# Graph convolutions on one Trainium2 core: a group's features are made behind the next tile's sums, and the slot products get a third PSUM bank

## The chip, the cores and the metric

The kernel runs on one core of a Trainium2 chip. The metric is device time in microseconds (us) of one execution. Before the change three runs took 6908.93, 6929.65 and 6957.83 us, so the median is 6929.65 us. Engines are called as in the profile: PE is the matrix engine (PEld its weight loads), DVE the vector engine, ACT the scalar engine, POOL the engine that issues the gathers, SP the engine that issues most plain DMAs.

## The reference, cut to what matters

There are 12500 nodes with 128 features and 200000 edges sorted by target. First an attention layer over the edges adds its result to `x`. Then three graph convolutions follow, each with the same edges; the change touches only these:

```python
def _gcn_conv(x, W, b, src, dst, norm, num_nodes):
    h = x @ W
    msg = h[src] * norm[:, None]
    out = jax.ops.segment_sum(msg, dst, num_segments=num_nodes)
    return out + b
...
h = _gcn_conv(x, W1, b1, src, dst, norm, n)
h = _batch_norm(jax.nn.relu(h), g1, beta1)
h = _gcn_conv(h, W2, b2, src, dst, norm, n)
h = _batch_norm(jax.nn.relu(h), g2, beta2)
h = _gcn_conv(h, W3, b3, src, dst, norm, n)
return _batch_norm(h, g3, beta3)
```

`norm` is the product of one factor per source and one per target node, and each node has an edge to itself. The first convolution widens to 256 features (`W1` is 128x256), the others have 128. The batch norm needs mean and variance over all nodes, so a convolution must be finished before the next starts.

## The kernel before

The first half of the time (up to about 3560 us of the profiled span) is the attention; while it runs, the edges are also sorted into slots. Then come the three convolutions (`convolutions`, L1389), each one call of `run` in `conv_slots` (L1239). All matrices are fp32; each fp32 matrix product is two matmul records in the trace.

**Tiles and blocks.** Target nodes are cut into 106 tiles of 118. Nine tiles are a block (`TB`), so there are 12 blocks. Source nodes are cut into 98 segments of 128, and 14 segments are a take-group (`SG`), so a block has 7 take-groups. For each tile and segment there are 13 slots, that is, up to 13 edges from that segment into that tile; the edges that find no slot (up to 768 a tile) are fetched row by row.

**take(b)** (L1264) fills the slots of block b. For each take-group, in sub-groups of 4, 4, 4 and 2 segments, DVE builds a one-hot matrix `go` (L1273, three buffers), PE multiplies it with the segment's features, which lie in SBUF (`gp`, L1276, two PSUM banks), and ACT copies the product to `stage` (L1278, two buffers). When a take-group is done, two DMAs on ACT's queue write it to a block `m` in DRAM (L1280).

**reduce(b)** (L1283) adds up a block's tiles. For each tile three DMAs on SP's queue bring its slots back, now with the slots as partitions (`mr`, L1297, loaded three tiles ahead, four buffers); six gathers on POOL fetch the rows of the slotless edges (`rows`, L1312, by the helper in L150, five buffers); DVE builds the one-hot matrix `oh` of their targets (L1316, two buffers); and PE adds 10 products of `mr` (L1320) and 6 of `rows` (L1322) into a part of the PSUM tile `zp`, after one product of the tile's own rows `tg` with an identity (`own`, L1195).

**finish** (L1191) walks through a group of three tiles (`GN`) that share one `zp` bank. After the third tile DVE multiplies `zp` by the target factors into `zt` (L1199), and `use` makes the group's features of it. In the first convolution `use1` (L1398) multiplies `zt` on PE with both halves of W1 (L1403, 2 products of 354 columns, so four records), ACT adds the bias and applies relu (L1404, twice), DVE takes statistics (L1344, twice), and a DMA on ACT's queue stores the second half (`hb_d`, L1406). In the second and third convolution `use` (L1409) is one ACT instruction that reads `zt` (L1411) and one statistics instruction.

**Order.** Take-groups of block b alternate with the tiles of block b-1: the loop in L1328 gives `reduce` 0, 1, 3, 5, 6, 8 and 10 steps by the end of take-group 0 to 6, where the first step only issues loads. So the written order is: take-group, then one or two tiles, and so on; the third tile of a block's last group comes at the end of the block. What each engine really runs is not exactly the written order. A planner in the framework takes the written order as the priority and its own guess of durations, and lays out one fixed order for each engine. In the trace, for example, 12 `gp` matmuls stand between matmuls of one tile's sum.

**PSUM before.** [...]one constant (`tb`), two each for `gp`, `zp` and `bank` (the pool `ps`, L1246; `bank` is used by the products with W1 and by the transforms between convolutions). Seven are taken.

Of the kernel before, what the change touches and what calls it, by code (L numbers as in the profile page):

```python
# [8 lines left out]
FP = mybir.dt.float32  # L9
# [5 lines left out]
PSUM = bass.MemoryType.PSUM  # L15
# [3 lines left out]
D = 128  # L19
# [15 lines left out]
TN = 118  # L35
# [14 lines left out]
def tile_gnn(ctx: ExitStack, tc: tile.TileContext, x, src, dst, ea, eaT, wqkvT, weT, w1, w2, w3, par, out):  # L50
# [102 lines left out]
    with ExitStack() as s:  # L153
        once = s.enter_context(tc.tile_pool(name="once", bufs=1))
        sr = s.enter_context(tc.tile_pool(name="sr", bufs=3))
        ps = s.enter_context(tc.tile_pool(name="ps", bufs=2, space=PSUM))
# [507 lines left out]
    def fast():  # L664
# [234 lines left out]
        with ExitStack() as s:  # L899
# [7 lines left out]
            wk = s.enter_context(tc.tile_pool(name="wk", bufs=2))  # L907
# [280 lines left out]
                              dinv_d[t0 * TN:(t0 + n) * TN].unsqueeze(0).to_broadcast([P, n * TN]))  # L1188
            return tg, db

        def finish(wk, t0, n, zp, use, ps, own_, add):  # L1191

            tg, db = own_
            for i in range(n):
                nc.tensor.matmul(zp[:, i, :], tg[:, i, :], ident[:TN, :TN], start=True, stop=False)  # L1195
                add(i)
                yield
            zt = wk.tile([P, GN * TN], FP, name="zt")
            nc.vector.tensor_tensor(zt[:, :n * TN], zp[:, :n].rearrange("p a b -> p (a b)"), db[:, :n * TN],  # L1199
                                    op=ALU.mult)  # L1200
            use(wk, t0, n, zt[:, :n * TN], ps)

        def pools(s, *names):
            return [s.enter_context(tc.tile_pool(name=n, bufs=b)) for n, b in names]
# [4 lines left out]
        def conv_rows(s):  # L1209


            ew, ga, wk = pools(s, ("ew", 1), ("ga", 3), ("wk", 2))
            ps = s.enter_context(tc.tile_pool(name="ps", bufs=2, space=PSUM))
            srcA = ew.tile([P, NTT, JJ], I32, name="srcA")
            dlA = ew.tile([P, NTT, JJ], BF, name="dlA")
            nc.sync.dma_start(srcA, sw_d.rearrange("t (p j) -> p t j", j=JJ))
            nc.sync.dma_start(dlA, dlb_d.rearrange("t (p j) -> p t j", j=JJ))

            def run(table, use, ready):
                for g in range(NS // SG):  # L1220
                    ready(g)
                for t0, n in groups(NTT, GN):
                    zp = ps.tile([P, GN, TN], FP, name="zp")

                    def add(i):
                        rows = ga.tile([P, JJ, D], FP, name="rows")
                        for j in range(JJ):
                            gather(rows[:, j, :], table, srcA[:, t0 + i, j:j + 1])
                        oh = wk.tile([P, JJ, TN], FP, name="oh")
                        one_hot(oh, dlA[:, t0 + i, :])  # L1230
                        for j in range(JJ):
                            nc.tensor.matmul(zp[:, i, :], rows[:, j, :], oh[:, j, :], start=False, stop=(j == JJ - 1))

                    for _ in finish(wk, t0, n, zp, use, ps, own(wk, table, t0, n), add):
                        pass

            return ps, run

        def conv_slots(s):  # L1239
# [4 lines left out]
            blocks = s.enter_context(tc.tile_pool(name="blocks", bufs=3, space=DRAM))  # L1244
            tb = s.enter_context(tc.tile_pool(name="tb", bufs=1, space=PSUM))
            ps = s.enter_context(tc.tile_pool(name="ps", bufs=2, space=PSUM))  # L1246
            nums = tb.tile([P, TN], FP, name="nums")
            nc.vector.tensor_copy(nums, iota_f[:, :TN])
            TS = TB * SB

            def run(table, use, ready):
                every = [(b, g) for b in range(NBK) for g in range(NS // SG)]
                gis = []

                def load_slots(k):

                    for b, g in every[len(gis):k]:
                        gi = gy.tile([P, TB, SG * SB], U8, name="gi")
                        nc.sync.dma_start(gi.rearrange("p t k -> p (t k)"),
                                          gi_d[b, g].rearrange("t k -> (t k)").unsqueeze(0)  # L1260
                                          .to_broadcast([P, TS * SG]))
                        gis.append(gi)

                def take(b, m):  # L1264
                    for g in range(NS // SG):
                        load_slots(b * (NS // SG) + g + 2)
                        if b == 0:
                            ready(g)
                        stage = sg.tile([TS, SG, D], FP, name="stage")
                        gv = gis[b * (NS // SG) + g].rearrange("p t (s k) -> p s t k", k=SB)  # L1270
                        for a, n in groups(SG, 4):
                            go = gx.tile([P, 4, TB, SB], FP, name="go")
                            nc.vector.tensor_scalar(go[:, :n], gv[:, a:a + n], iota_q, None, op0=ALU.is_equal)  # L1273
                            gp = ps.tile([TS, 4, D], FP, name="gp")
                            for i in range(n):
                                nc.tensor.matmul(gp[:, i, :], go[:, i].rearrange("p t k -> p (t k)"),  # L1276
                                                 hs[:, g * SG + a + i, :], start=True, stop=True)
                            nc.scalar.copy(stage[:, a:a + n, :], gp[:, :n, :])  # L1278
                        for x, y in ((0, 112), (112, TS)):
                            nc.scalar.dma_start(m[x:y, g * SG:(g + 1) * SG, :], stage[x:y])  # L1280
                        yield

                def reduce(b, m):  # L1283

                    tiles = range(b * TB, min(NTT, (b + 1) * TB))
                    mrs, owns = {}, {}

                    def load(t):
                        if t not in tiles:
                            return  # L1290
                        if t % GN == 0:
                            owns[t] = own(wk, table, t, min(GN, NTT - t))
                        k = (t - b * TB) * SB
                        mv = m[k:k + SB].rearrange("k s d -> (k s) d")
                        mr = mrs[t] = mt.tile([P, RC, D], FP, name="mr")
                        for x, y, r in ((0, 112, RC), (112, LP, RC), (LP, LP + 1, LR)):
                            nc.sync.dma_start(mr[x:y, :r], mv[x * RC:(y - 1) * RC + r]  # L1297
                                              .rearrange("(p c) d -> p c d", c=r))

                    for a in range(AH):  # L1300
                        load(tiles[0] + a)
                    yield
                    for t0 in range(tiles[0], tiles[-1] + 1, GN):
                        n = min(GN, NTT - t0)
                        zp = ps.tile([P, GN, TN], FP, name="zp")

                        def add(i):
                            t = t0 + i
                            load(t + AH)
                            rows = ga.tile([P, JO, D], FP, name="rows")  # L1310
                            for j in range(JO):
                                gather(rows[:, j, :], table, srcO[:, t, j:j + 1])  # L1312
                            mr = mrs.pop(t)
                            oh = wk.tile([P, RC + JO, TN], FP, name="oh")
                            sh = list(oh.shape)
                            nc.vector.tensor_tensor(oh, nums.unsqueeze(1).to_broadcast(sh),  # L1316
                                                    dlS[:, t, :].unsqueeze(2).to_broadcast(sh), op=ALU.is_equal)
                            for j in range(RC):
                                q = LP + (j < LR)
                                nc.tensor.matmul(zp[:, i, :], mr[:q, j, :], oh[:q, j, :], start=False, stop=False)  # L1320
                            for j in range(JO):
                                nc.tensor.matmul(zp[:, i, :], rows[:, j, :], oh[:, RC + j, :], start=False,  # L1322
                                                 stop=(j == JO - 1))

                        yield from finish(wk, t0, n, zp, use, ps, owns.pop(t0), add)

                taken = None
                for b in range(NBK + 1):  # L1328
                    tiles = reduce(b - 1, taken) if b else iter(())
                    if b < NBK:  # L1330
                        taken = blocks.tile([TS, NS, D], FP, name="m")
                        done = 0
                        for g, _ in enumerate(take(b, taken)):
                            while done < g * (TB + 1) * SG // (NS - SG):
                                next(tiles, None)
                                done += 1
                    for _ in tiles:
                        pass

            return ps, run  # L1340

# [161 lines left out]
```

## Time and profile before

| | |
|---|---|
| median of 3 runs | 6929.65 us (6908.93 to 6957.83) |
| profiled execution | 6996.49 us; its span from the first to the last instruction is 6994.6 us |
| mean granted PE clock over the span | 0.762 |
| PE busy / DVE / ACT / POOL | 64% / 47% / 22% / 50% of the span |
| first convolution | about 3560 to 4640 us of the span |
| second, with the transform of its input | about 4650 to 5790 us |
| third, with the transform of its input | about 5810 to 6920 us |

The profile is one execution; each row of it gives busy time and the idle time of an engine just before the instructions of a row, with what ended most of that idle time. "issue" means that the engine waited for nothing that the profile shows. "remote", or "another core or an unknown queue", means that the wait ended with a semaphore's update for which no instruction was found near in time; there is only one core here. Ends of matmuls are modelled, their starts are recorded. The DMA column is the mean busy share of the core's 16 DMA engines.

### The profile page before, as it was taken

What the parts mean: (1) busy time and instruction counts of PE and PEld (TensorE: products, weight loads), DVE (VectorE), ACT (ScalarE), POOL (GpSimd) and SP (SyncE); (2) the same over time, 40 slices, a digit from 0 to 9 for tenths busy, and PEclk for the clock granted to TensorE, in tenths of its full rate; (3) what the DMA queues carried; (4) which work ended last, traced back from release to release, by engine and by line L of the source; (5) the groups of instructions that cost most, each with busy time, mean ns of one, the idle gap of its engine ahead of it and who ended that gap; (6) DMA issues with size and microseconds to landing.
All of it is one profiled execution on the core that took longest, in us unless ns stands there. A gap on an engine that the chain in (4) does not pass through costs nothing.

```text
span 6994.6 us, 79497 instructions
## 1 busy us (share of the span) xinstructions
PE 4480.9 (64%) x28140; PEld 4142.4 (59%) x28140; DVE 3297.8 (47%) x6145; ACT 1521.5 (22%) x2637; POOL 3518.1 (50%) x3617
## 2 busy tenths in 40 slices
PE   5455555555555555566557777786777776777776
PEld 2455544544444545555557777776777676767775
DVE  7344445565655666557523333352333334333334
ACT  2222222332222322222211211111111111111110
POOL 1444545455454554556435555525555553555552
PEclk9666666666666666667678888898888888888887
DMA  6434443433333433434377777766777776777776
GB/s 179 108 94 109 107 110 101 102 103 97 94 102 93 105 98 103 104 100 115 76 183 211 200 204 202 206 204 188 197 198 198 193 198 179 200 200 195 194 202 160
DMA packets 617743, 1051.02 MB, mean 150 GB/s; under 512 B 191467, under 2 KB 432043, under 8 KB 617233
## 3 DMA queue, kind: packets, MB, share of 16 engines
q1 hardware_dynamic: 434383, 478.08, 27.5%
q0 software_dynamic: 142608, 348.39, 19.0%
q10 hardware_dynamic: 40348, 219.37, 9.1%
q8 instruction: 228, 3.74, 0.2%
q14 instruction: 176, 1.44, 0.1%
HBM read 773.19 MB, written 272.26 MB: 149 GB/s over the span
## 4 chain that ended last, share of the span: by engine, by line
PE 41%; another core or an unknown queue 19%; DVE 16%; issue 12%; DMA 4%; ACT 2%; POOL 1%; SPq 1%; DVEq 0%; ACTq 0%; POOLq 0%
PE gp L1276 12%; PE zp L1320 10%; PE zp L1322 5%; PE qe L1061 5%; PE acc L1120 5%; DVE sc L1065 2%; DVE vals L1110 2%; DVE A L717 2%; DVE kv L1062 2%; DVE oh L1116 1%; PE sm L1072 1%; DVE A L718 1%; ACT stage L1278 1%; PE bank L1382 1%
## 5 line engine op out<-in xcount | busy, mean ns | idle before, releaser
L150 POOL DMA_INDIRECT rows<-t_d,srcO x1908 | 1834.9, 962 | 1605.8 <-issue 492.5
L150 POOL DMA_INDIRECT kv<-kv_d,srcA x1696 | 1678.9, 990 | 1638.1 <-DVE vals L1110 891.2
L1276 PE MATMUL gp<-hs,go 128*117 128x128 f32 x7056 | 1042.1, 305 | 553.3 <-issue 261.8
L1276 PEld LDWEIGHTS gp<-hs,go 128*117 128x117 f32 x7056 | 953.6, 207 | 613.9 <-issue 391.4
L1061 PE MATMUL qe<-qt,oht 128*128 128x128 f32 x3392 | 855.6, 418 | 581.3 <-DVE kv L1062 408.8
L1061 PEld LDWEIGHTS qe<-qt,oht 128*128 128x128 f32 x3392 | 769.8, 309 | 637.5 <-issue 381.5
L1278 ACT COPY stage<-gp 117x512 f32<-117x512 f32 x1008 | 514.4, 534 | 2442.7 <-PE gp L1276 823.1
L1316 DVE TENSOR_TENSOR oh<-nums,dlS 128x1888 f32<-128x1888 f32 x318 | 674.2, 2120 | 755.7 <-PE zp L1320 313.7
L1320 PE MATMUL zp<-oh,mr 128*128 128x118 f32 x6360 | 904.3, 288 | 182.8 <-issue 141.4
L1320 PEld LDWEIGHTS zp<-oh,mr 128*128 128x128 f32 x6360 | 834.2, 204 | 217.2 <-issue 189.0
L1273 DVE TENSOR_SCALAR go<-gi,iota_q 128x468 f32<-128x468 uint8 x1008 | 441.6, 460 | 931.4 <-remote 359.7
L1120 PE MATMUL acc<-vals,oh 128*118 128x137 f32 x3392 | 559.7, 335 | 175.4 <-ACT vals L1112 102.4
L1120 PEld LDWEIGHTS acc<-vals,oh 128*118 128x118 f32 x3392 | 538.0, 230 | 196.5 <-ACT vals L1112 116.6
L1322 PE MATMUL zp<-oh,rows 128*128 128x118 f32 x3816 | 531.4, 286 | 49.6 <-issue 42.2
L1322 PEld LDWEIGHTS zp<-oh,rows 128*128 128x128 f32 x3816 | 492.4, 202 | 57.8 <-issue 50.1
L1062 DVE TENSOR_TENSOR kv<-qe,kv 128x512 f32<-128x512 f32 x424 | 286.5, 679 | 329.7 <-remote 212.8
L1072 PE MATMUL sm<-wbd,ebx 128*128 128x32 f32 x848 | 211.4, 383 | 190.8 <-issue 71.2
L1072 PEld LDWEIGHTS sm<-wbd,ebx 128*128 128x128 f32 x848 | 211.9, 327 | 186.6 <-issue 124.6
L1116 DVE TENSOR_TENSOR oh<-nums,dlA 128x1888 f32<-128x1888 f32 x106 | 223.9, 2113 | 198.7 <-PE qe L1061 89.3
L1054 ACT ACTIVATE oht<-dw_b,niota 128x2048 f32<-128x2048 bf16 x106 | 212.2, 2002 | 388.9 <-remote 200.0
L1099 PE MATMUL sm<-ident,run 8*128 8x8 f32 x212 | 57.1, 340 | 321.1 <-DVE run L1095 177.6
L1099 PEld LDWEIGHTS sm<-ident,run 8*128 8x128 f32 x212 | 47.2, 275 | 343.8 <-DVE run L1095 187.4
(246 smaller groups left out, 3994.7 us busy)
## 6 DMA issues: line engine op xcount, KB each, us to landing
m<-stage ACTq DMA_DIRECT2D x252, 784.0 KB
mr<-m SPq DMA_DIRECT2D x318, 560.0 KB
dw_b<-dlb_d SPq DMA_DIRECT2D x106, 512.0 KB
gi<-gi_d SPq DMA_DIRECT2D x252, 204.8 KB
rows<-t_d,srcO POOLq DMA_INDIRECT x1908
kv<-kv_d,srcA POOLq DMA_INDIRECT x1696
ebx<-in_edge_attrT_dram SPq DMA_DIRECT2D x106, 256.0 KB
mr<-m SPq DMA_DIRECT2D x318, 75.0 KB
```

What stands on the lines that cost most here:

```text
L150: nc.gpsimd.indirect_dma_start(out=o, out_offset=None, in_=table[:, :], in_offset=bass.IndirectOffsetOnAxis(ap=idx, axis=0))
L1061: nc.tensor.matmul(qe[:, k, :], ohv[:, :, j + k], qt, start=True, stop=True)
L1062: nc.vector.tensor_tensor(qk[:, j:j + 4, :], qe, qk[:, j:j + 4, :], op=ALU.mult)
L1072: nc.tensor.matmul(bias[:, 4 * k:4 * k + 4, :].rearrange("p j h -> p (j h)"), eb.rearrange("a (p k) -> a k p", k=4)[:, k, :], wbd, start=T ...
L1116: nc.vector.tensor_tensor(oh, nums.unsqueeze(1).to_broadcast(sh), dlA[:, t, :].unsqueeze(2).to_broadcast(sh), op=ALU.is_equal)
L1120: nc.tensor.matmul(acc, oh[:, j, :], va[:, j, :], start=(j == 0), stop=(j == JJ - 1))
L1273: nc.vector.tensor_scalar(go[:, :n], gv[:, a:a + n], iota_q, None, op0=ALU.is_equal)
L1276: nc.tensor.matmul(gp[:, i, :], go[:, i].rearrange("p t k -> p (t k)"), hs[:, g * SG + a + i, :], start=True, stop=True)
L1278: nc.scalar.copy(stage[:, a:a + n, :], gp[:, :n, :])
L1316: nc.vector.tensor_tensor(oh, nums.unsqueeze(1).to_broadcast(sh), dlS[:, t, :].unsqueeze(2).to_broadcast(sh), op=ALU.is_equal)
L1320: nc.tensor.matmul(zp[:, i, :], mr[:q, j, :], oh[:q, j, :], start=False, stop=False)
L1322: nc.tensor.matmul(zp[:, i, :], rows[:, j, :], oh[:, RC + j, :], start=False, stop=(j == JO - 1))
```

## The change

`finish` gets a list `later`. At the end of a group it still issues the multiplication into `zt`, but instead of calling `use` it puts the call on the list. The call is taken off the list in the next group's first step, after that tile's `own` product, loads, gathers, `oh` and sums have been issued. Across a block's end the next group's first step lies in the next block, behind that block's first three take-groups. Each convolution takes the last call off the list at its end. `conv_rows`, a branch that this input doesn't take, is changed in the same way.

Besides, `gp` leaves the pool `ps` for a pool `pg` of its own with three buffers. PSUM then has one bank of constants, three for `gp`, two for `zp` and two for `bank`, which makes eight.

```diff
-        def finish(wk, t0, n, zp, use, ps, own_, add):
+        def finish(wk, t0, n, zp, use, ps, own_, add, later):
             tg, db = own_
             for i in range(n):
                 nc.tensor.matmul(zp[:, i, :], tg[:, i, :], ident[:TN, :TN], start=True, stop=False)
                 add(i)
+                while later:
+                    later.pop()()
                 yield
             zt = wk.tile([P, GN * TN], FP, name="zt")
             nc.vector.tensor_tensor(zt[:, :n * TN], zp[:, :n].rearrange("p a b -> p (a b)"), db[:, :n * TN],
                                     op=ALU.mult)
-            use(wk, t0, n, zt[:, :n * TN], ps)
+            later.append(lambda: use(wk, t0, n, zt[:, :n * TN], ps))
...
             ps = s.enter_context(tc.tile_pool(name="ps", bufs=2, space=PSUM))
+            pg = s.enter_context(tc.tile_pool(name="pg", bufs=3, space=PSUM))
...
-                gis = []
+                gis, later = [], []
...
-                            gp = ps.tile([TS, 4, D], FP, name="gp")
+                            gp = pg.tile([TS, 4, D], FP, name="gp")
...
-                        yield from finish(wk, t0, n, zp, use, ps, owns.pop(t0), add)
+                        yield from finish(wk, t0, n, zp, use, ps, owns.pop(t0), add, later)
...
                     for _ in tiles:
                         pass
+                later.pop()()
```

## The prediction, made before the changed kernel ran

> **What bounds the kernel now.** The change touches the convolutions alone, so I first asked for busy time and DMA share over 900 us from the middle of each:
>
> ```profile
> core 0: us, PE busy (x) PEld busy (x) DVE busy (x) ACT busy (x) POOL busy (x), PEclk, DMA share, GB/s
> 3700.00:4600.00 900.00, 691.01 (x5118) 650.74 (x5118) 349.42 (x459) 174.83 (x339) 518.47 (x538) 0.88 0.74 205
> 4800.00:5700.00 900.00, 665.66 (x4978) 634.75 (x4978) 327.48 (x425) 158.87 (x307) 512.25 (x533) 0.86 0.72 197
> 5900.00:6800.00 900.00, 664.09 (x4973) 633.64 (x4972) 331.00 (x430) 158.72 (x308) 517.70 (x539) 0.86 0.74 198
> ```
>
> No engine is full. PE is the nearest: 5118 matmul records at a pitch of some 0.111 us (twenty follow each other in 2.2 us in the timeline) are 568 of 900 us. The pace is the same in all three: the same windows hold 279, 277 and 278 ACT copies of L1278, at 28 a block, that is 90.3, 91.0 and 90.6 us a block. That is odd, because the first convolution has the products with W1 on PE and the others do not. I come back to it.
>
> Next, what PE waited for in the three convolutions:
>
> ```profile
> PE gp L1276 <- issue: 257.4, 114, 15.9
> PE gp L1276 <- ACT stage L1278: 194.8, 68, 15.3
> PE zp L1320 <- issue: 141.4, 229, 10.6
> PE gp L1276 <- DVE go L1273: 62.3, 19, 6.2
> PE zp L1322 <- issue: 42.2, 54, 1.8
> PE bank L1403 <- DVE zt L1199: 41.9, 16, 11.6
> ```
>
> (line, what it waited for, us in total, times, longest). Both parts of the change have a row: PE waits 194.8 us for ACT to empty a `gp` bank, and for `zt` before L1403. The group row of the first convolution has that second wait whole, 89.2 us:
>
> ```profile
> L1403 PE MATMUL bank<-zt,w1s 128*128 128x354 f32 x136 | 61.6, 585 | 89.2 <-DVE zt L1199 40.9 <-issue 26.1 <-DVE go L1273 22.2
> ```
>
> The timeline of one group end shows how it comes about:
>
> ```profile
> 3907.49 1.50 PE L1322 MATMUL zp<-oh,rows 128*128 128x118 f32 x12
> ...
> 3908.83 1.06 PE L1320 MATMUL zp<-oh,mr 128*128 128x118 f32 x8
> ...
> 3912.52 0.53 DVE L1199 TENSOR_TENSOR zt<-zp,db 128x354 f32<-128x354 f32 x1 [4.02 <-remote]
> ...
> 3912.96 2.12 DVE L1316 TENSOR_TENSOR oh<-nums,dlS 128x1888 f32<-128x1888 f32 x1
> ...
> 3913.10 1.46 PE L1403 MATMUL bank<-zt,w1s 128*128 128x354 f32 x4 [3.21 <-issue]
> ...
> 3914.99 0.46 DVE L1273 TENSOR_SCALAR go<-gi,iota_q 128x468 f32<-128x468 uint8 x1
> ```
>
> The group's last sums started at 3907.49 and are over by 3909.0, yet `zt` started at 3912.52, though DVE was free. PE had eight matmuls of the next tile to do and then stood for 3.2 us. So PE's results reach the others late, and L1403 makes PE wait for its own news.
>
> How late shows at the end of a block, where the loads of three tiles are issued together:
>
> ```profile
> 3955.00:3960.00 5.00, 3.88 (x33) 3.71 (x33) 2.51 (x3) 0.96 (x2) 2.53 (x4) 1.00 0.18 51
> 3960.00:3965.00 5.00, 3.15 (x20) 2.32 (x18) 3.01 (x3) 0.00 (x0) 3.78 (x5) 1.00 0.93 244
> 3965.00:3970.00 5.00, 1.35 (x10) 1.17 (x10) 1.30 (x3) 1.60 (x3) 3.78 (x5) 0.92 0.97 251
> 3970.00:3975.00 5.00, 0.00 (x0) 0.00 (x0) 0.00 (x0) 0.00 (x0) 2.50 (x3) 0.50 0.98 250
> ```
>
> (columns as in the first table). While the DMA engines are at 0.93 to 0.98, PE, DVE and ACT fall silent together, and the clock drops to 0.50. In the timeline `gp` matmuls from 3966.3 are followed by ACT's copy at 3975.6. Such a stretch is not a want of work.
>
> **The change part by part.** *The deferred features, first convolution.* There are 36 groups, three a block. I followed each L1403 in the timeline. For a block's first group PE stands about 3.3 us; afterwards it does 8 matmuls of the tile, then `gp`, which must wait for the `go` at 3914.99. With L1403 behind the tile's sums, PE can do the tile's other 12 + 12 matmuls meanwhile, and L1403 still fits ahead of that `go`. What is won is the 4 of L1320 and 12 of L1322 that now follow the `gp`: 16 x 0.111 = 1.8 us. For the second group the `gp` behind L1403 have their `go` already, so the 3.3 us are won. For the third PE stands about 1.5 us, but 2 us later comes the block end's wait of about 8 us, which swallows it. That makes 12 x (1.8 + 3.3) = 61 us. Against this stands the equal pace: without L1403 (61.6 busy and 89.2 us of waiting, some 12 us a block) the second convolution is no faster. Its `zt` waits on DVE are longer instead, 143 us for 36 against 80 us. So part of what is won at one wait comes back at the next. I take half, 30 us; the ends are 0 and 89.
>
> *The other two convolutions.* Here L1411 (0.59 us on ACT) and one statistics instruction move. The planner has put L1411 where `zt` is done, with no other ACT work ready, and it will do so again. `zt` itself doesn't move, and DVE still waits there with `oh` and `go` behind it. I count nothing. The cover is ACT's idleness (159 of 900 us busy); if copies were held behind L1411 today, its own waits of 139.0 ("issue") and 92.5 us (for `zt`) bound the gain. But 92.5 in 6 waits with a longest of 32 lie at the convolutions' ends, so I put the upper end at 40.
>
> *What else is moved.* Two ACT instructions (0.56 us each), two statistics (0.52 us each) and the store of `hb_d` (0.35 us on ACT's queue) pass one tile's `oh` (2.1 us on DVE), its loads on SP and gathers on POOL. SP's and POOL's order stays, as `use` has nothing there. The store goes later relative to the DMAs of L1280; its data are read only a convolution later. The new wait: L1403 still waits for `zt`, now with a tile's sums ahead. Queued behind it are `gp` and the next sums; by then `zt` is some 3 us old, so nothing. `zt` has two buffers and one new one a group, so holding it a tile longer blocks nobody. The last group of a block is used after three take-groups of the next; only a convolution's end needs it, and there it is taken at once as today.
>
> *The third `gp` bank.* PE may run one sub-group further ahead of ACT: eight matmuls, 8 x 0.109 = 0.87 us. The 68 waits for ACT average 2.9 us, so each can shrink by that: 59 us. "TensorE: Matmul & The Clock Gate" of the Trainium skill speaks against it in its section on HAM oscillation: of a kernel whose waits for loads had been restructured away it says "Adding PSUM double-buffering gave no further gain". By that this term is 0; by the row it is 59, and the row is for this kernel, with the wait named. The lower end is 0, since `go` also has three buffers, whose release waits for the same late news of PE. The upper end adds the 114 "issue" waits at 0.87 us, 99 more.
>
> *Is a silent stretch cured by buffers at all?* The same skill's page "SBUF — State Buffer", section on who interferes with whom, says that DMA never contends with a compute engine. By it the silent stretches are dependencies and more buffers could remove most of gp's 257.4 us too. The rows say that all three engines stop just when DMA share is near 1 with PE's results outstanding. I go by the rows: a buffer saves 0.87 us of such a stretch and no more.
>
> The sum: 30 + 59 = 89 us off 6996.5 us, the profiled execution, leaves 6907; in proportion to the median, 6929.65 x 6907/6996.5 = 6841. I predict 6840 us.
>
> **The rivals.** *No difference (6900 to 6950; 0.27).* Pace is set by the bursts of loads and PE's late news; what PE does earlier it waits for later. For it: three equal paces with unequal PE work. Against: PE does stand at L1403 and at full banks in between bursts.
>
> *More than forecast (about 6680; 0.13).* The whole 89 at L1403, 59 + 99 at the banks come to 247 us: 6929.65 x (1 - 247/6996.5) = 6685. For it: shorter stops keep the clock, which averages 0.87. Against: the equal pace.
>
> *Slower, by the planner's order on PE (about 7050; 0.25).* With three banks the planner lets three sub-groups of `gp` pass before it turns to sums. PE works in order: where the third `gp` has no `go` yet, because DVE stands at `zt`, ready sums are stuck behind it. Today the four-matmul pieces of L1320 between the `gp` fill such holes. The price is about one `go` round (0.46 us plus a 0.6 us handover) at each of 108 groups, and twice that where an `oh` of 2.1 us is in the way: about 120 us, 6929.65 x (1 + 120/6996.5) = 7048. It decides once gp's wait for `go`, 62.3 us now, grows by more than the 89 us won.
>
> *It does not do what it says.* The planner may put L1403 back before the sums, since it becomes ready at `zt`. Then the first term is 0 and the second remains: 6929.65 x (1 - 59/6996.5) = 6871; I count it with the forecast and the null.
>
> **How the numbers follow.** The forecast has 0.35, more than forecast 0.13, the null 0.27, slower 0.25. A measurement of this kernel can tell about 1% from no change, so faster means below 6860. Forecast and better make 0.48 faster, the null 0.27, slower 0.25. The range goes from 6685 to 7000: above it lies the worse half of the slower case, below it the tail of the better one. Faster cases alone would span 6685 to 6875.
>
> **What would show it.** Right: L1403's idle before it in the first convolution falls from 89 to under 20 us; ACT's row under gp's waits falls from 194.8 to about 135; copies in 900 us rise from 278 to about 286. Wrong: DVE's waits at `zt` (80, 143 and 142 us) or gp's waits for `go` grow by what was won, or the 900 us windows again hold 278. A `gp` run of 24 matmuls in PE's timeline with a wait inside it would speak for the slower case.

## The result, and the profile after

The changed kernel takes 7178.01 us (median of 4 runs, 7142.36 to 7191.49); the kernel before, with a further run beside it, 6919.29 us. The ratio is 1.0349, with an interval of 1.0315 to 1.0383. The forecast was 1.3% less; it became 3.5% more. The profiled execution took 7191.49 us, its span 7189.2 us, at a mean granted PE clock of 0.743 (0.762 before).

All of the loss is in the convolutions. From the first `gp` to the last gathered row the trace of before has 3375 us, that of after 3598 us, so 223 us more. Here are windows of 900 us from the middle of each convolution of the kernel after (columns as in the first table of the prediction):

```profile
3700.00:4600.00 900.00, 695.49 (x4883) 650.03 (x4881) 324.47 (x434) 163.59 (x320) 491.47 (x515) 0.84 0.71 196
4900.00:5800.00 900.00, 654.11 (x4550) 617.00 (x4550) 301.28 (x389) 144.93 (x283) 469.68 (x491) 0.81 0.67 180
6100.00:7000.00 900.00, 656.76 (x4610) 617.01 (x4608) 303.07 (x394) 145.88 (x284) 470.23 (x491) 0.82 0.67 181
```

In the first convolution PE is as busy as before by its time (695 for 691 us) with fewer matmuls (4883 for 5118). The granted clock is lower in all three (0.84, 0.81, 0.82 for 0.88, 0.86, 0.86), and the DMA share has not risen, it has fallen (0.74, 0.72, 0.74 before). ACT's copies of `gp` number 262, 255 and 257 where the prediction looked for 286 and before had 279, 277 and 278; at 28 a block that is 96.2, 98.8 and 98.1 us a block. The same work takes all engines longer.

Next, what PE waited for in the three convolutions after the change (in the rows: us in total, times, longest; L1282 is the `gp` of L1276 before, L1284 its copy on ACT, L1326 and L1328 the sums of L1320 and L1322):

```profile
PE gp L1282 <- issue: 382.3, 294, 12.3
PE zp L1326 <- issue: 278.6, 401, 2.4
PE gp L1282 <- ACT stage L1284: 126.3, 52, 6.4
PE gp L1282 <- DVE go L1279: 49.4, 19, 22.1
```

The groups of the first convolution after the change are the products with W1 (L1403 before) and `zt` (L1199 before):

```profile
L1410 PE MATMUL bank<-zt,w1s 128*128 128x354 f32 (+1 forms) x144 | 53.1, 482 | 11.6 <-DVE zt L1202 10.3 <-issue 1.3
...
L1202 DVE TENSOR_TENSOR zt<-zp,db 128x354 f32<-128x354 f32 (+1 forms) x36 | 18.7, 520 | 168.5 <-PE zp L1326 95.4 <-PE gp L1282 39.4 <-PE zp L1196 12.6
```

Both waits that the change aims at did shrink: the one ahead of the products with W1 from 89.2 to 11.6 us, the one for a free `gp` bank from 194.8 to 126.3 us. That is 146 us of waiting gone. In their place the "issue" waits of `gp` rose from 257.4 to 382.3 us, those of the sums from 141.4 to 278.6 us, together by 262 us, and in the first convolution `zt` waits 168.5 us on DVE where it waited 80.

The part of the page that shows where time and loss stand side by side is one that the prediction didn't open: the group of the gathers on POOL, first before, then after (x instructions, busy us, mean ns, then the idle time just before them and what ended it).

```profile
L150 POOL DMA_INDIRECT rows<-t_d,srcO x1908 | 1834.9, 962 | 1605.8 <-issue 492.5 <-PE zp L1195 377.5 <-PE gp L1276 275.2
```

```profile
L150 POOL DMA_INDIRECT rows<-t_d,srcO x1908 | 1825.7, 957 | 1836.7 <-PE zp L1328 576.1 <-issue 518.9 <-PE zp L1196 448.9
```

POOL issues the same 1908 gathers in the same time, and stands 231 us longer ahead of them, mostly until PE frees their buffers. So the time in which gathers are issued is fixed, and the added time lies in the rest. I worked that out from the starts of the gathers in the traces: each start plus 1.4 us (they follow each other every 1.25 us) is "gather time", and what is left of the convolutions is "rest". PE's matmul records are counted in each, without the 594 of the transforms between convolutions.

| trace | convolutions, us | gather time | rest | PE records in gather time, per us | in the rest, per us |
|---|---|---|---|---|---|
| before | 3375 | 2453 | 922 | 13820, 5.63 | 4192, 4.55 |
| after | 3598 | 2434 | 1164 | 12625, 5.19 | 5387, 4.63 |

The sum closes: after the change PE does 1195 fewer records in gather time, and at 4.63 a us they take 258 us later on, for the 242 us that the rest has grown. In the rest PE is no faster but slower: of it, 334 of 922 us before and 699 of 1164 us after were granted at half clock, where the records follow each other at 0.213 us and not at 0.111. It also holds the starts and ends of the convolutions, some 230 us in both. So the table says where the time is; it doesn't say that gathers are the cause. The question for the experiments is therefore not which wait is shorter, but what holds PE to 4.6 to 5.6 records a us, when twenty in a row take 2.2 us, or 9 a us.

One group end in the timeline after the change shows what a stretch of gathers looks like (start us, us, engine, what, and in brackets the idle time before):

```profile
4044.18 2.79 PE L1282 MATMUL gp<-hs,go 128*117 128x128 f32 x24
...
4047.02 0.77 PE L1410 MATMUL bank<-zt,w1s 128*128 128x354 f32 x2
...
4049.81 0.59 ACT L1284 COPY stage<-gp 117x512 f32<-117x512 f32 x1 [12.19 <-remote]
...
4050.45 0.70 PE L1282 MATMUL gp<-hs,go 128*117 128x128 f32 x4 [2.66 <-issue]
...
4053.62 0.95 POOL L150 DMA_INDIRECT rows<-t_d,srcO  x1 [0.31 <-issue]
...
4055.53 0.59 ACT L1284 COPY stage<-gp 117x512 f32<-117x512 f32 x1 [5.12 <-remote]
...
4056.16 5.47 PE L1282 MATMUL gp<-hs,go 128*117 128x128 f32 x24 [5.01 <-issue]
```

PE runs all 24 records of three `gp` sub-groups, which three banks now allow. The first sub-group is done after some 0.9 us, yet ACT, idle for 12 us, gets to copy it only at 4049.81, 5.6 us after the run began. The next copy waits until 4055.53, after the last gather of the stretch has been issued at 4053.62. This is the late news that the prediction saw at 3907 and took for an effect of the loads of slots. Gathers run here, but loads of slots do too (the DMA share counts as 1.02 to 1.03 between 4044 and 4050), so this stretch alone can't tell the two apart. After its pause of 5 us PE needs 5.47 us for 24 records that took 2.79 us before: the granted clock was 1.00 in the first run and 0.50 in the second.

### The profile page after: what moved, and what is told of

Same layout as the page of the kernel before. It is cut to its first block, busy times and chain, and to the rows that moved or that the text cites. A ratio compares the mean times of both kernels' runs of the same rounds, so it can differ in the third digit from the quotient of the medians.

```text
span 7189.2 us, 79526 instructions
## 1 busy us (share of the span) xinstructions
PE 4671.0 (65%) x28140; PEld 4274.6 (59%) x28140; DVE 3288.4 (46%) x6145; ACT 1515.7 (21%) x2637; POOL 3518.0 (49%) x3617
## 4 chain that ended last, share of the span: by engine, by line
PE 47%; another core or an unknown queue 16%; issue 15%; DVE 13%; DMA 3%; ACT 3%; SPq 1%; POOL 1%; ACTq 0%; DVEq 0%; POOLq 0%
PE gp L1282 12%; PE zp L1326 11%; PE zp L1328 7%; PE acc L1120 6%; PE qe L1061 5%; DVE sc L1065 2%; DVE vals L1110 1%; PE sm L1072 1%; DVE kv L1062 1%; DVE A L717 1%; DVE oh L1116 1%; PE zp L1196 1%; PE bank L1389 1%; DVE A L718 1%
## 5 line engine op out<-in xcount | busy, mean ns | idle before, releaser
L1282 PE MATMUL gp<-hs,go 128*117 128x128 f32 x7056 | 1055.2, 304 | 592.3 <-issue 382.3
L1282 PEld LDWEIGHTS gp<-hs,go 128*117 128x117 f32 x7056 | 956.0, 206 | 673.0 <-issue 494.0
L1326 PE MATMUL zp<-oh,mr 128*128 128x118 f32 x6360 | 963.6, 298 | 318.2 <-issue 278.6
L1326 PEld LDWEIGHTS zp<-oh,mr 128*128 128x128 f32 x6360 | 880.6, 213 | 365.0 <-issue 333.2
L1284 ACT COPY stage<-gp 117x512 f32<-117x512 f32 x1008 | 516.5, 534 | 2609.8 <-PE gp L1282 1024.3
L1279 DVE TENSOR_SCALAR go<-gi,iota_q 128x468 f32<-128x468 uint8 x1008 | 425.4, 449 | 1232.7 <-remote 505.5
L1322 DVE TENSOR_TENSOR oh<-nums,dlS 128x1888 f32<-128x1888 f32 x318 | 674.2, 2120 | 599.0 <-PE zp L1328 417.7
L1120 PE MATMUL acc<-vals,oh 128*118 128x137 f32 x3392 | 581.3, 339 | 247.3 <-issue 138.1
L1328 PE MATMUL zp<-oh,rows 128*128 128x118 f32 x3816 | 599.4, 311 | 39.5 <-issue 37.2
L1328 PEld LDWEIGHTS zp<-oh,rows 128*128 128x128 f32 x3816 | 560.7, 226 | 58.0 <-issue 54.2
L1202 DVE TENSOR_TENSOR zt<-zp,db 128x354 f32<-128x354 f32 x108 | 56.2, 520 | 483.8 <-PE zp L1328 199.4
L1110 DVE TENSOR_TENSOR vals<-kv,sm 128x2048 f32<-128x2048 f32 x106 | 241.6, 2279 | 15.4 <-ACT sm L1109 15.4
```

What stands on the lines that cost most here:

```text
L1110: nc.vector.tensor_tensor(vh[:, :, :, :C], kv[:, :, D:].rearrange("p j (h c) -> p j h c", h=H), ex.unsqueeze(3).to_broadcast([P, JJ, H, C] ...
L1120: nc.tensor.matmul(acc, oh[:, j, :], va[:, j, :], start=(j == 0), stop=(j == JJ - 1))
```

## The experiments

The runs met chips of two kinds, and no number below can be understood without that: on some, the kernel before takes about 6940 us, as above (called chips with late updates), on others about 5150 us (chips with even updates). The names come from the semaphore updates by which PE tells the other engines that a result is ready, PE's "news"; they are counted under "Without gathers". Each ratio is against the kernel before on the same chip. The theories are the *prediction's* (late news comes with bursts of loads, and each part gains a little or nothing), the *order* rival (three banks let the planner make long `gp` runs, behind which ready sums are stuck), and, as the traces suggest, *gathers* (while POOL's gathers run, PE's semaphore updates reach the others late).

### One part at a time

Features deferred, `gp` left with two banks:

```diff
-            pg = s.enter_context(tc.tile_pool(name="pg", bufs=3, space=PSUM))
...
-                            gp = pg.tile([TS, 4, D], FP, name="gp")
+                            gp = ps.tile([TS, 4, D], FP, name="gp")
```

> The deferral alone, gp back to two PSUM banks. Two theories of the 3.5% (about 240 us). Order theory: the third bank is the whole cost, because with it the planner's order on PE has gp runs of 12 and 14 products instead of 6 and 8; then the deferral alone is the small gain that the prediction took for it, 6860 to 6925 us (0 to -1%). Deferral theory: moving use behind the next tile's sums is the cost (PE's and ACT's later work meets full buffers); then this kernel is at 7100 us or more (+2.5 to +3.5%).

Third bank, features not deferred:

```diff
+            pg = s.enter_context(tc.tile_pool(name="pg", bufs=3, space=PSUM))
...
-                            gp = ps.tile([TS, 4, D], FP, name="gp")
+                            gp = pg.tile([TS, 4, D], FP, name="gp")
```

> The third gp bank alone, use called at once as before. Order theory: nearly all of the loss is here, 7110 to 7190 us (+3 to +4%). Deferral theory: 6860 to 6930 us, the bank's own small gain. If both edits cost something by themselves, each stands at +1 to +2%.

Third bank, but `go` with two buffers, which in the planned order on PE breaks the runs of `gp` up again (2 to 8 products in place of mostly 12 and 14):

```diff
-... ("gx", 3), ...
+... ("gx", 2), ...
```

> Third gp bank, use at once, and only two go buffers, which in the planned order on PE brings back short gp runs (mostly 2 to 8 products). Order theory: most of the loss is gone again, 6900 to 7000 us, although there is a buffer less. If instead the bank itself costs (a buffer more, whatever the order), it stays at 7100 us or above, and the missing go buffer can only add to it.

These three met a chip with even updates (before 5157.03 us) and measured 5159.05 us, 1.000 (0.9991 to 1.0009); 5154.01 us, 0.9996 (0.9989 to 1.0003); and 5150.42 us, 0.998 (0.9971 to 0.9989). So on such a chip neither part matters, and the null rival holds to 0.2%. The windows of the third bank alone there, one from each convolution:

```profile
2600.00:3400.00 800.00, 734.03 (x6004) 703.28 (x6003) 411.21 (x584) 193.12 (x376) 551.50 (x574) 0.97 0.94 266
...
3450.00:4250.00 800.00, 693.42 (x5706) 675.22 (x5705) 385.77 (x519) 176.72 (x340) 580.79 (x604) 0.94 0.90 250
4300.00:5000.00 700.00, 619.01 (x5149) 605.31 (x5148) 336.82 (x440) 165.21 (x318) 531.34 (x554) 0.95 0.94 262
```

The DMA engines are at 0.90 to 0.94, PE does 7.1 to 7.5 records a us, and of 2592 us of convolutions 2413 are gather time. The gathers are nearly the whole length; PE keeps up. The mean DMA share is *higher* than the 0.72 to 0.74 of the kernel before on the other kind, and PE seldom falls silent: cut into stretches of 5 us, this trace has 346 with a DMA share of 0.93 or more, and 7 of them hold ten PE records or fewer. In the first trace of before it is 53 of 187, but also 76 of the 488 stretches with less traffic. So a DMA share near 1 is not enough to silence PE.

The same was then run on chips with late updates, first the changed kernel again, unaltered:

> The changed kernel itself, beside the kernel before. In the last runs the kernel before took 5157 us and not 6929, and PE's semaphore updates came evenly (none closer than 0.15 us, no heap at 1.4 us), where in the first profiles they came late and in clumps. Theory that the 3.5% belong to late updates: where the updates are even, this kernel is within 0.3% of the kernel before, as each edit alone was; where they are late again (kernel before near 6900 us), it is 3 to 4% slower. Theory that the loss is in the combination of both edits whatever the updates do: +2 to +3.5% here too, although each edit alone cost nothing.

Third bank alone:

> The third gp bank alone, once more. With even updates: within 0.3% of the kernel before, as it was. With late updates (kernel before near 6900 us) the order theory says that it carries nearly the whole loss, +3 to +4%; the deferral theory says 0 or below.

Features deferred alone:

> The deferral alone again, wanted on a chip with late updates (kernel before near 6940 us). There the third bank alone cost 3.25% and both edits 3.7%. Order theory: the deferral alone, with the short gp runs of two banks, is within 1% of the kernel before: +0.45% if the two edits simply add, down to -0.5% if the 89 us of waiting at L1403 count for anything. Deferral theory, weakened already: above +1.5%. With even updates (before near 5157 us): within 0.2%, as before.

Third bank with two `go` buffers:

> Third gp bank with two go buffers again: the planned gp runs are mostly 2 to 8 products instead of 12 and 14. With late updates: the order theory expects most of the 3.25% to be gone, 6920 to 7010 us (-0.3 to +1%), although the kernel has a buffer less. If a third bank costs by itself, or if every loss of a hand-over's buffer costs, it stays at +3% or more. With even updates: -0.2%, as before.

| edit | us | before | ratio |
|---|---|---|---|
| the whole change | 7193.55 | 6940.77 | 1.037 (1.0352 to 1.0388) |
| third bank alone | 7167.79 | 6940.77 | 1.0325 (1.03 to 1.035) |
| deferral alone | 7054.16 | 6936.75 | 1.0169 (1.0135 to 1.0202) |
| third bank, two `go` | 7160.23 | 6936.75 | 1.0333 (1.0299 to 1.0367) |

Each part alone costs, the bank 227 us, the deferral 117 us; together 253 us, less than their sum. So neither theory on record, all of it in the bank or all of it in the deferral, holds. PE's waits in the convolutions with the deferral alone were:

```profile
PE gp L1281 <- issue: 300.4, 134, 11.0
PE gp L1281 <- ACT stage L1283: 265.0, 74, 32.6
PE zp L1325 <- issue: 169.3, 299, 5.7
```

With the third bank alone they were:

```profile
PE gp L1277 <- issue: 349.4, 263, 6.6
PE zp L1321 <- issue: 234.9, 314, 9.4
PE gp L1277 <- ACT stage L1279: 118.9, 46, 6.8
PE gp L1277 <- DVE go L1274: 86.4, 28, 24.2
```

With the third bank and two `go` buffers they were:

```profile
PE gp L1277 <- issue: 428.0, 191, 10.6
...
PE gp L1277 <- ACT stage L1279: 243.4, 54, 10.6
PE gp L1277 <- DVE go L1274: 173.2, 67, 23.4
```

With the deferral the wait ahead of the products with W1 shrinks (to 16.0 us), and waiting for ACT grows (194.8 to 265.0 us). With the bank, that wait shrinks and the "issue" waits grow. In the last kernel the runs of `gp` were planned short again, the "issue" waits of the sums fell to 29.8 us, and the loss stayed at 3.3%: the waits have other names. The order rival had put this kernel at 6920 to 7010 us, so this speaks against it. But it has one `go` buffer less as well, so it does not settle it.

Gather time is 2437, 2432 and 2438 us in these three traces (2453 before). PE's records a us in it are 5.37, 5.15 and 5.19 (5.63 before), and the rest of the convolutions 1050, 1159 and 1134 us (922 before). In all of them gather time is the same, PE does less in it, and the rest is longer.

### Without gathers

All but the first 18 of the 1908 gathers are left out, and the sums use the first gathered rows again and again. This leaves work out: the slotless edges are not added rightly. PE, DVE and ACT run the same instructions in the same order in the traces. PE no longer waits for gathered rows, but that had cost it only 7.1 us.

```diff
-                            rows = ga.tile([P, JO, D], FP, name="rows")
-                            for j in range(JO):
-                                gather(rows[:, j, :], table, srcO[:, t, j:j + 1])
+                            if not fixed:
+                                fixed.append(ga.tile([P, JO, D], FP, name="rows"))
+                                for j in range(JO):
+                                    gather(fixed[0][:, j, :], table, srcO[:, t, j:j + 1])
+                            rows = fixed[0]
```

> The kernel before, but the convolutions gather the rows of the slotless edges for the first tile only and use them for all tiles; PE's, DVE's and ACT's instructions and PE's planned order are the same. Left out: 1890 of 1908 gathers. In the trace of before, PE's semaphore updates come in late clumps, and the clumps end with the gathers' own completions. If the gathers hold PE's news back, the convolutions fall from about 90 us a block to 60 to 70, that is 6000 to 6300 us in all. If the bursts of slot loads hold them back (as the prediction read it), only the DMA share of the gathers goes: 6750 to 6900 us.

On the chip with even updates it took 4884.03 us, 0.946 (0.9442 to 0.9479), 273 us less. The same edit was then run on a chip with late updates, in the kernel before and in that with the third bank alone:

> The kernel before without 1890 of its 1908 gathers in the convolutions (the rows of the first tile are used for all), same order on PE. With late updates: if the gathers hold PE's news back, as the heap of updates at 1.4 us that ends with the gathers' completions suggests, the convolutions lose most of their excess and the kernel falls by 600 to 1000 us. If they only take DMA time, it falls by 200 to 300 us, as it did with even updates (4884 against 5157 us).

> The same cut of gathers in the kernel with the third bank alone, its order on PE unchanged (long gp runs). If the long runs cost only because PE's news is late, and the gathers make it late, it is within 0.7% of the kernel before without gathers. If the long runs cost whatever the news does, the distance of 3% (some 200 us) to that kernel remains.

Here it is 5899.29 us, 0.8518 (0.848 to 0.8556), from the kernel before: 1037 us less. The third bank without gathers takes 5862.29 us, 0.8474 (0.8435 to 0.8514). Windows of the first of these two, one from each convolution, and its `gp` group:

```profile
3600.00:4300.00 700.00, 667.00 (x5674) 647.90 (x5673) 377.69 (x524) 188.28 (x366) 0.00 (x0) 0.99 0.80 234
4500.00:5100.00 600.00, 566.80 (x4962) 560.65 (x4961) 335.77 (x458) 149.74 (x294) 0.00 (x0) 0.98 0.81 235
5200.00:5700.00 500.00, 473.81 (x4193) 469.15 (x4194) 269.72 (x356) 131.76 (x258) 0.00 (x0) 0.99 0.84 241
```

```profile
L1276 PE MATMUL gp<-hs,go 128*117 128x128 f32 x7056 | 878.3, 277 | 77.8 <-DVE go L1273 40.9 <-DMA gi<-gi_d 30.6 <-ACT stage L1278 5.9
```

The DMA share rises from 0.74 to 0.80 to 0.84, and yet PE is busy 94 to 95%, at a granted clock of 0.98 to 0.99. Waiting for ACT falls from 194.8 to 5.9 us and "issue" is gone from the row. The convolutions take 2310 us, and 2325 us on the chip with even updates: without gathers the two kinds of chip are alike there. Of 184 stretches of 5 us with a DMA share of 0.93 or more, 4 are silent, where it was 53 of 187. And the chip was still of the late kind: the attention, which kept its own gathers in this run, took 3516 us (3544 in the first trace of before, 2491 on the even kind), and its updates still came in clumps. This settles that the late news goes with the gathers and not with DMA share as such. What in a gather does it, its issue on POOL or its small packets, is not told apart.

Without gathers the third bank gains: 5862.29 against 5899.29 us, 37 us or 0.6%; the two intervals overlap a little (0.8435 to 0.8514 and 0.848 to 0.8556), so its sign is likely rather than shown. That is the size of the prediction's 59 us, in a kernel whose news isn't late. So the 3.25% that the bank costs on this kind of chip need the gathers.

The semaphore updates of PE, counted in the convolutions by their distance in time, say the same:

| trace | updates | under 0.05 us | 0.15 to 0.3 us | 1.38 to 1.48 us |
|---|---|---|---|---|
| before, late kind | 7142 | 3103 | 1206 | 599 |
| without gathers, late kind | 7444 | 0 | 6071 | 3 |
| third bank, even kind | 7771 | 0 | 6171 | 11 |

Before has clumps with gaps between them, the others have not. In the first trace, half of the updates that end such a gap fall within 0.05 us of a gather's own update, 4.4 times as often as chance would have it; for all other DMAs it is 2.1 times.

### Half of the gathers

Three of a tile's six gathers, whose rows are used twice; the other half of the slotless edges gets wrong rows.

```diff
-                            for j in range(JO):
+                            for j in range(JO // 2):
...
-                                nc.tensor.matmul(zp[:, i, :], rows[:, j, :], oh[:, RC + j, :], start=False,
+                                nc.tensor.matmul(zp[:, i, :], rows[:, j % (JO // 2), :], oh[:, RC + j, :], start=False,
```

> The kernel before with three of six gathers a tile (PE multiplies the first three for the other three again, so its work and order are unchanged). Left out: half of the gathers of the convolutions. In the trace of before the convolutions take 3375 us: 2453 us in which gathers run (PE 5.6 records a us) and 922 us without (4.6), and without any gathers 2310 us. If gather time and PE's lost progress go together: half the gather time is 1225 us with 6900 records, the other 11100 at the 7.9 a us of the run without gathers take 1410 us, in all 2640, so the kernel falls by about 735 us to 6200. If POOL's time were the bound as such, it would fall by up to 1070 us and no further than the run without gathers (5900 us). With even updates: 4890 to 4950 us beside 5157.

> Half of the gathers left out, PE's work and order as before. With late updates: about 6200 us if the lost progress goes with the time in which gathers run (working: half of 2453 us of gathers with 5.6 records a us, the other 11100 records at 7.9 a us). With even updates: 4955 us, as before.

Both runs met the even kind: 4954.84 us, 0.963 (0.9614 to 0.9646), and 4958.87 us, 0.9635 (0.9604 to 0.9666). Half of the gathers are worth 192 us there, nearly all of them 273 us: so leaving out the second half brings only 81 us more. That would fit PE as the next bound, which was 94 to 95% busy without gathers on the other kind; no run here shows it. How the loss on the late kind grows with the number of gathers stays open.

### A finer order

A take-group is cut in two, so that slots and sums alternate twice as finely, once with two banks and once with three.

```diff
                             nc.scalar.copy(...)
+                            if a == 4:
+                                yield
...
-                            while done < g * (TB + 1) * SG // (NS - SG):
+                            while done < g * (TB + 1) // 13:
```

> Third gp bank, use at once, and the written order is finer: reduce gets its steps after every second sub-group and not after a whole take-group, so that on PE whole tiles of sums lie between gp runs of mostly 6 to 10 products, with three go buffers kept. So far, with late updates: third bank +3.25%, third bank with two go buffers +3.3%, deferral +1.7%; without the gathers the third bank costs nothing (-0.5%). Order theory: what PE finds to do while gathers hold its news back decides, so this order is within 1% of the kernel before or faster (6800 to 7000 us beside 6937). If it is the bank as such, it stays at +3% (7130 us or more). With even updates: within 0.5%.

> The same finer written order with two gp banks, all else as before. Nothing is added or taken away, only the order on the engines differs. Order theory, with late updates: the time moves by more than 1% one way or the other, most likely faster by 0 to 3% (6730 to 6940 us), as gp and sums mix more evenly. If only buffers count and order does not, it is within 0.5% of the kernel before. With even updates: within 0.5%.

> Third gp bank with the finer written order again, wanted on a chip with late updates (kernel before near 6940 us). Order theory: within 1% of the kernel before or faster, 6800 to 7000 us. If the bank costs as such: +3%, 7130 us or more. With even updates: -0.1%, as before.

> Two banks with the finer written order again, nothing else changed. Order theory, with late updates: moves by more than 1% one way or the other, most likely faster by 0 to 3%. If only buffers count: within 0.5%. With even updates: +0.3%, as before.

> Third gp bank with the finer written order. With late updates: order theory within 1% of the kernel before or faster (6800 to 7000 us); bank theory +3% (7130 us or more). With even updates: -0.1%, as twice before.

> Two banks with the finer written order, nothing else changed. With late updates: order theory more than 1% one way or the other, most likely faster by 0 to 3%; buffers theory within 0.5%. With even updates: +0.3%, as twice before.

All six runs met the even kind (before 5151.04, 5146.71 and 5153.24 us). Three banks took 5144.88, 5140.12 and 5148.89 us, ratios 0.9989, 0.9988 and 0.9989 (intervals within 0.998 to 0.9998). Two banks took 5162.66, 5160.31 and 5165.2 us, ratios 1.0029, 1.0032 and 1.0024 (within 1.0013 to 1.0043). So there the third bank is worth 0.4% under the finer order, and nothing under the old one (0.9996). But whether a finer order helps where the change lost was not measured, and with it the question of order against buffers stays open. No kernel that computes everything beat the one before on the late kind; on the even kind the finer order with three banks beats it by 0.1%, and the third bank with two `go` buffers by 0.2%.

## Why the prediction was wrong

**What bounds the kernel.** This step failed, and the others rest on it: it took the silent stretches for an effect of bursts of loads, and in both terms of the forecast a wait of PE that shrinks could only win time or nothing (lower ends of 0). "No engine is full" was right, and the equal pace of the three convolutions was noticed, but its cause was not looked for. It was in the profile's page: a block has 9 x 6 = 54 gathers at 1.25 us, some 68 of its 90 us, in all three convolutions alike. The silent stretches were ascribed to the DMA share near 1 beside which one of them stood. Leaving out the gathers took 1037 us off while DMA share rose. The clock was named only as a possible gain; that pauses cost matmuls at half clock was put at nothing.

Here the Trainium skill was weighed. The prediction set the page "SBUF — State Buffer", section on who interferes with whom (DMA does not contend with a compute engine; the section is about access to SBUF), against the rows, and went by the rows. They did show that the engines fall silent, but not that bandwidth was the cause: at 0.90 to 0.94, on the other kind of chip, PE ran at 7.1 to 7.5 records a us. "Adding PSUM double-buffering gave no further gain", from the section on HAM oscillation of "TensorE: Matmul & The Clock Gate", came nearer the result than the row for the bank, yet on the late kind the bank did worse than nothing (+3.25%).

**The deferred features, 30 us won.** The stall went as told (89.2 to 11.6 us, forecast under 20). Its worth was wrong in sign: alone the deferral costs 1.7%. The clause "part of what is won at one wait comes back at the next" was right in kind and too small: with the deferral alone ACT's row grows by 70 us and the "issue" waits by 43 and 28 us. The lower end of 0 for this term was wrong: it was reasoned that moved work costs nothing while it has cover, and here PE's rate in gather time fell from 5.63 to 5.37 records a us.

**The third bank, 59 us won.** ACT's row went to 126.3 us with both edits (forecast about 135) and to 118.9 us with the bank alone, so that wait came out as told, though not quite as worked: it was to shrink by 0.87 us at each of 68 waits, and 52 waits are left, of 2.4 us on average where it was 2.9. The step from a shrunken wait to time won failed. Alone the bank costs 227 us; the "issue" waits took over. They had been put among the possible gains (99 us) and never among the places where the time could go. The lower end of 0 failed here too.

**The slower rival (7050, 0.25).** It had the sign, and its long runs came: the two of 24 records in the timeline above have no wait inside, which its other mark asked for. Its mark did not: it should decide once gp's wait for `go` grows from 62.3 by over 89 us, and that wait fell to 49.4 us. And with short runs and two `go` buffers the loss was the same 3.3%. So its mechanism is not shown, and that it lay nearer to 7178 us than the forecast did is luck.

**The null (0.27)** was wrong on the kind of chip of this result and right to 0.2% on the other kind, though not for its reason: there the gathers set the length, with PE keeping up. **It does not do what it says** was wrong: the products with W1 follow sums of the next tile in the trace.

**The marks.** Right: the idle time at L1403, ACT's row, and "DVE's waits at `zt` grow" as a sign of failure (80 to 168.5 us in the first convolution; over all three 365 to 484 us). Wrong: the copies in 900 us.

**What is still open.** Why either edit lowers PE's rate in gather time, from 5.63 records a us to 5.37 with the deferral and 5.15 with the bank. Fewer, longer runs of `gp` in the planned order (366 runs after, 468 before) could explain the bank, but not the deferral, which hardly alters them (458), nor the kernel with two `go` buffers (492). The traces show where the time is, not why. In PE's stream the time beyond 0.112 us a record is 1314 us before and 1535 us after, 221 of the 223 us. Some 67 us of that are records at half clock, 0.213 us apart: half clock was granted for 931 us of the convolutions before and for 1276 us after. Some 155 us are pauses of over 0.3 us. They differ in kind. Pauses of 1.25 to 1.5 us, about one gap between clumps of updates, number 53 before and 51 with the deferral alone, but 146 with the third bank alone and 154 with both (73 us before, 212 us with both). The deferral alone and the bank with two `go` buffers have more time instead in pauses of over 2.5 us (595 us before, 646 and 814 us). So the kernel with two `go` buffers loses its time in another way than the one with long runs, which is one reason more why it can't decide the order rival. Whether the lower clock only follows from the pauses was not tested.

## What to carry to other kernels

A wait that disappears is not yet time won: find the part of the stage whose length is fixed (here some 2435 us of gathers), and ask whether the edit lets more work be done beneath it. Count also at which clock the work left over will run. When a consumer stands idle long after its producer has finished, look for what holds the news back, by leaving out one suspected traffic at a time, before buffers are added or work is moved around it. Before a few per cent are put down to an edit, see that the kernel before is the same on the chip where it is tried.

## What was not expected of the hardware

The same program took 5157 us on one chip and 6940 us on another. Which kind a chip is, nothing but its runs told; why, stays open. On the slower kind PE's semaphore updates arrive in clumps (some 43 ns apart) after gaps of about 1.41 us where gathers run. A gather's own pace is no different: 1.25 us a piece (0.95 busy, 0.30 issue), 2434 us of gather time after the change and 2413 us with the third bank on the faster kind. Without gathers the slower kind runs the convolutions in 2310 us and the faster one in 2325 us.
